# A convolution with a mixture of experts and an attention layer: normalising in two phases, and routing gates kept on chip

## The chip, the cores and the metric

The kernel runs on one core of one Trainium2 chip. The metric is the time of one launch on the device in microseconds (us), the median of several runs.

## What is computed

The input x is 32 images of 128 channels and 56 x 56 pixels, all in float32. Layer 0 is a block with a mixture of experts; layer 1 a 3 x 3 convolution (dilation 3), an attention over channels in the frequency domain and a gated branch. Cut to what matters here:

```python
# layer 0
x = depthwise_conv_7x7(input) + dw_bias                      # NCHW -> NHWC
x = (x - mean) / sqrt(var + 1e-6) * ln_gamma + ln_beta       # over the 128 channels
xf = x.reshape(T, C)                                         # T = 32*56*56 = 100352 tokens
topv, topi = top_k(xf @ Wg + bg, 2)                          # 8 experts, two for each token
wts = softmax(topv)
# each expert takes its cap = 1.25*T/8 tokens of highest wts[:, 0]; other pairs are dropped
y = gelu(xf[slot] @ W1[e] + b1[e]) @ W2[e] + b2[e]           # for every kept pair
moe = sum over the kept pairs of a token of  y * wts
x = input + x + layer_scale * moe
# layer 1
feat = gelu(batchnorm(conv3x3(x)));  F2 = fft2(feat)
attn = softmax of the channels' correlations in 8 heads
y = concat(|ifft2(attn @ F2)|, |ifft2(sigmoid(gate net of F2.real) * F2)|) + x
```

## The kernel before

**Convolution stage.** The images are taken in 8 groups of four. A group has 98 token columns of 128 tokens each (TG = 98; J = 784 columns in all), and its convolution is 16 steps `conv(g, c0, y)` of 8 channels. Each step loads an image tile `xt` (784 KB) and a weight tile `wt` (448 KB) from SyncE's queue (three buffers each), does 64 matmuls into two PSUM banks `psa`, and VectorE moves the banks into `y` with the bias added (L144). One group's `y` is [128 tokens, 98, 128 channels], with two buffers.

The rest of layer 0's work on a group, its normalising, its logits and its choice of experts, runs behind the convolution of the next group. `block` cuts the 98 columns into six blocks of 16 and one of 2, and gives five phases for each:

- `stats`: mean and variance on VectorE, a square root on ScalarE;
- `norm`: one ScalarE activation for every column (L181), then the affine part, a multiplication by gamma and an addition of beta on VectorE (L185), then the DMA of the token rows to the DRAM tensor `xf`, issued from ScalarE's queue (L188);
- `across`: TensorE transposes the columns (L196, tile `pyt`), ScalarE copies them to `yT`;
- `logits`: the matmul with Wg (tile `plq`), and ScalarE's copy;
- `back`: transposes back (tile `pl`), VectorE adds the bias into `lg`.

`plan` sets the order by hand: phase i of block b is issued after convolution step 3b/2 + i (rounded down) of the next group, and `choose` one step after the last phase, at step 14:

```python
for i, phase in enumerate(block(g, y, lg, t0, n)):
    at.setdefault(b * 3 // 2 + i, []).append(phase)
...
at[last + 1] = [lambda: choose(g, lg)]
```

Phases of a step follow the step's convolution in every engine's queue. After the last group they run without a convolution: the drain. `choose(g, lg)` finds the two best experts of every token and their weights, and writes `key`, which the search for the experts' thresholds reads. It also fills a tile `meta` with the two weights and the first expert's number, and stores it by DMA (L299) behind the tokens' rows: a row of `xf` has PITCH = 144 floats, 128 of them the token, 16 for `meta`, of which three are used.

**Expert stage.** First VectorE and TensorE search the thresholds (L416, L445) and make the list `ids` of expert 0's tokens; the later experts' searches and lists run in small pieces (`tick`) beside the experts. A chunk is 512 tokens, 31 chunks to an expert. `fetch` gathers the rows of the next chunk with four indirect DMAs of GpSimd (L671, tile `xg`, four buffers), TensorE transposes them (L677), and VectorE works out the chunk's gate with three small operations (L682, L690: which of the row's two weights belongs to expert e) and copies the transposes to `xT` (L691). `expert` does the two matmuls (L705 and L715) with the gelu between them (L708); VectorE adds b2 (L728) and multiplies by the gate (L734) into `yo`, which SyncE's queue stores to `yf`, a row for each slot.

**Layer 1.** Images go in 16 pairs; `front` makes the layer's input and its 3 x 3 convolution for the next pair while `back` transforms the present one. A row block `r` is 7 columns of 128 tokens (112 row blocks). `feed` places row block r, sums r + 1 and gathers r + 3. `gather(r)` loads the tokens' rows `xs` from `xf` (L845) and gathers the rows of both slots from `yf` into two tiles `y` with 14 indirect DMAs of GpSimd (L850, four buffers, that is, two row blocks). `total(r)` adds both to `xs`; `place` transposes the sum (L872) and adds it to the image (L877).

```python
def total(r):
    ...
    for y in ys:
        nc.vector.tensor_tensor(out=xs, in0=xs, in1=y, op=ALU.add)
```

The functions that the change touches, and their callers:

Of the kernel before, what the change touches and what calls it, by code (L numbers as in the profile page):

```python
# [37 lines left out]
C = 128  # L38
# [6 lines left out]
E = 8  # L45
# [9 lines left out]
CB = 8  # L55
PITCH = 144
BIG = 1.0e30
# [14 lines left out]
def conv_seq_kernel(ctx: ExitStack, tc: tile.TileContext, t: dict, out: bass.AP, dbg: dict):  # L72
# [28 lines left out]

    xf = dram.tile([J * 128, PITCH], F32, name="xf")
    yf = dram.tile([NSLOT + 1, C], F32, name="yf")
    xfv = xf.rearrange("(j p) c -> p j c", p=128)

    rkey = tc.tile_pool(name="rkey", bufs=1)
    rk = rkey.__enter__()
# [4 lines left out]
    with tc.tile_pool(name="a1", bufs=1) as a1, tc.tile_pool(name="a2", bufs=2) as a2, tc.tile_pool(  # L114
# [36 lines left out]
        def block(g, y, lg, t0, n):  # L151
# [26 lines left out]
            def norm():  # L178
                for i in range(n):
                    yi = y[:, t0 + i, :]  # L180
                    nc.scalar.activation(  # L181
                        yi, yi, AF.Identity, scale=sd[:, i : i + 1], bias=nb[:, i : i + 1]
                    )
                for w, op in ((gB, ALU.mult), (bB, ALU.add)):
                    nc.vector.tensor_tensor(  # L185
                        out=yb, in0=yb, in1=w.unsqueeze(1).broadcast_to([128, n, C]), op=op
                    )
                nc.scalar.dma_start(out=xfv[:, g * TG + t0 : g * TG + t0 + n, :C], in_=yb)  # L188

# [59 lines left out]

            return [stats, norm, across, logits, back]  # L250

        def choose(g, lg):
# [33 lines left out]
            m1, e1 = tops  # L286
            meta = a1.tile([128, TG, PITCH - C], F32, name="meta", tag="meta")
            nc.gpsimd.memset(meta, 0.0)  # L288
            w1, w2 = meta[:, :, 0], meta[:, :, 1]
            nc.vector.tensor_tensor(out=e1, in0=e1, in1=m1, op=ALU.subtract)  # L290
# [6 lines left out]
            nc.vector.tensor_tensor(out=w2, in0=e1, in1=m1, op=ALU.mult)  # L297
            nc.vector.tensor_copy(meta[:, :, 2], firsts[0][:, cut])
            nc.scalar.dma_start(out=xfv[:, cut, C:], in_=meta)  # L299
            hot = hots[0]  # L300
# [9 lines left out]

        NS = C // CB
        sizes = [16] * (TG // 16) + ([TG % 16] if TG % 16 else [])

        def plan(g, y):
            lg = a2.tile([128, TG, E], F32, name="lg")
            at = {}
            t0 = 0
            for b, n in enumerate(sizes):
                for i, phase in enumerate(block(g, y, lg, t0, n)):
                    at.setdefault(b * 3 // 2 + i, []).append(phase)  # L320
                t0 += n
            last = max(at)
            at[last + 1] = [lambda: choose(g, lg)]
            return at
# [35 lines left out]
    with tc.tile_pool(name="b1", bufs=1) as b1, tc.tile_pool(name="b2", bufs=2) as b2, tc.tile_pool(  # L360
# [301 lines left out]
        def fetch(e, ids, c0):  # L662

            ns = min(512, cap - c0 * 128)
            xg = c4.tile([128, 4, PITCH], F32, name="xg")
            xT = c2.tile([C, 512], F32, name="xT")
            gates = []
            pt = bank("pxt")
            for q in range(-(-ns // 128)):
                n = min(128, ns - q * 128)  # L670
                nc.gpsimd.indirect_dma_start(  # L671
                    out=xg[:n, q, :],
                    out_offset=None,
                    in_=xf,
                    in_offset=bass.IndirectOffsetOnAxis(ap=ids[:n, c0 + q : c0 + q + 1], axis=0),
                )
                nc.tensor.transpose(pt[:, q * 128 : q * 128 + n], xg[:n, q, :C], ident[:n, :n])  # L677
            gate = c4.tile([128, 4], F32, name="gate")
            gat2 = c4.tile([128, 4], F32, name="gat2")
            for n, q in spans(ns):  # L680
                for to, i, op in ((gate, 0, ALU.is_equal), (gat2, 1, ALU.not_equal)):
                    nc.vector.scalar_tensor_tensor(  # L682
                        out=to[:n, q],
                        in0=xg[:n, q, C + 2],
                        scalar=float(E - e),
                        in1=xg[:n, q, C + i],
                        op0=op,
                        op1=ALU.mult,
                    )
                nc.vector.tensor_tensor(out=gate[:n, q], in0=gate[:n, q], in1=gat2[:n, q], op=ALU.add)  # L690
            nc.vector.tensor_copy(xT[:, :ns], pt[:, :ns])  # L691
            return ns, xT, gate

# [6 lines left out]

        def expert(e, c0, ns, xT, gate, tick):
            hT = c2.tile([C, FF // C, 512], F32, name="hT")
# [23 lines left out]
            for n, q in spans(ns):  # L726
# [5 lines left out]
                    op=ALU.add,  # L732
                )
                nc.vector.tensor_tensor(  # L734
                    out=yo[:n, q],
                    in0=yo[:n, q],
                    in1=gate[:n, q].unsqueeze(2).broadcast_to([n, nq, C]),
                    op=ALU.mult,
                )
# [101 lines left out]
    def gather(r):  # L841
        if r >= NRB:
            return
        xs = d3.tile([128, NB, C], F32, name="xs")
        nc.sync.dma_start(out=xs, in_=xfv[:, r * NB : (r + 1) * NB, :C])  # L845
        ys = []
# [12 lines left out]
    def total(r):  # L859
        if r >= NRB:  # L860
            return
        xs, ys = rows[r]
        for y in ys:
            nc.vector.tensor_tensor(out=xs, in0=xs, in1=y, op=ALU.add)  # L864
# [442 lines left out]
```

## Time and profile before

| what | us |
|---|---|
| median of three runs (5589.1 to 5595.3) | 5591.9 |
| the profiled execution | 6457.2 |
| its span, from the first to the last instruction | 6455.5 |
| convolution beside the blocks' phases | 0 to 952 |
| drain: phases of the last group | 952 to 1067 |
| first search and list | 1067 to 1204 |
| experts | 1204 to 3370 |
| layer 1 | 3370 to 6455 |

The profile is of one execution and is read in this way. The stages in the table are cut at their first and last instructions in the timeline. The engines are PE (TensorE; PEld is its weight load), DVE (VectorE), ACT (ScalarE), POOL (GpSimd) and SP (SyncE); a name with q, as ACTq, is an instruction on that engine's queue that issues a DMA or handles a semaphore. A group of instructions is given by line, engine, operation, the tiles written and read, the count, and then the busy time, the mean time of one in ns, and the idle time of the engine just before it with what released it. "L850 POOL ... <-DVE xs L864" says that the gathers stood until the sums in line 864 were done. A line of waits has the engine and line that waited, for what, the time in all, the number of waits and the longest. A DMA queue has its packets, megabytes, and the share of the 16 DMA engines' time that it took. "Another core or an unknown queue" and "remote" stand for a wait whose releaser the profile doesn't show.

### The profile page before, as it was taken

What the parts mean: (1) busy time and instruction counts of PE and PEld (TensorE: products, weight loads), DVE (VectorE), ACT (ScalarE), POOL (GpSimd) and SP (SyncE); (2) the same over time, 40 slices, a digit from 0 to 9 for tenths busy, and PEclk for the clock granted to TensorE, in tenths of its full rate; (3) what the DMA queues carried; (4) which work ended last, traced back from release to release, by engine and by line L of the source; (5) the groups of instructions that cost most, each with busy time, mean ns of one, the idle gap of its engine ahead of it and who ended that gap; (6) DMA issues with size and microseconds to landing.
All of it is one profiled execution on the core that took longest, in us unless ns stands there. A gap on an engine that the chain in (4) does not pass through costs nothing.

```text
span 6455.5 us, 85506 instructions
## 1 busy us (share of the span) xinstructions
PE 4925.6 (76%) x32850; PEld 3344.5 (52%) x32850; DVE 3087.3 (48%) x6927; ACT 2090.8 (32%) x3595; POOL 2616.6 (41%) x2564
## 2 busy tenths in 40 slices
PE   6666653598887989999984677777776876777678
PEld 5555552376665756766762344434444443444445
DVE  4676675565656655345221334434443443444346
ACT  2445543132232323333330223333332333333235
POOL 0000000344353435444436645565555545555450
PEclk8888885799999999999996778888887887888789
DMA  9999983122222222222233233333333333333331
GB/s 229 220 233 214 227 201 83 36 65 62 52 67 51 70 54 69 68 70 72 70 110 70 64 83 99 92 85 75 96 94 84 96 91 82 81 93 95 83 97 44
DMA packets 616216, 634.08 MB, mean 98 GB/s; under 512 B 166145, under 2 KB 540546, under 8 KB 611714
## 3 DMA queue, kind: packets, MB, share of 16 engines
q1 hardware_dynamic: 332418, 395.64, 22.2%
q0 software_dynamic: 81664, 175.18, 12.7%
q10 hardware_dynamic: 201728, 57.81, 4.6%
q8 instruction: 260, 4.26, 0.3%
q14 instruction: 146, 1.20, 0.1%
HBM read 454.98 MB, written 173.41 MB: 97 GB/s over the span
## 4 chain that ended last, share of the span: by engine, by line
PE 35%; issue 14%; another core or an unknown queue 12%; POOL 11%; DVE 6%; ACT 3%; DMA 3%; DVEq 0%; POOLq 0%; ACTq 0%; SPq 0%
PE pf L895 8%; PE py L715 7%; PE ph L705 6%; POOL xg L671 6%; PE pm L939 5%; POOL y L850 4%; PE pt L931 3%; DMA xg<-xf,ids 2%; PE pg L963 1%; PE pxt L677 1%; PE pxs L872 1%; PE pim L1030 1%; DVE junk L416 1%; ACT oa L1043 1%
## 5 line engine op out<-in xcount | busy, mean ns | idle before, releaser
L850 POOL DMA_INDIRECT y<-yf,slot x1568 | 1640.2, 1046 | 1324.5 <-DVE xs L864 816.1
L671 POOL DMA_INDIRECT xg<-xf,ids x984 | 964.9, 981 | 1393.6 <-PE pxt L677 531.0
L895 PE MATMUL pf<-xp,cw 128*64 128x448 f32 x4032 | 1029.3, 596 | 186.1 <-issue 185.4
L708 ACT ACTIVATE hT<-ph,b1t 128x512 f32<-128x512 f32 (+1 forms) x992 | 673.3, 682 | 1468.7 <-PE ph L705 1282.1
L715 PEld LDWEIGHTS py<-W,hT 128*128 128x128 f32 x7872 | 951.5, 195 | 251.5 <-ACT hT L708 124.8
L715 PE MATMUL py<-W,hT 128*128 128x128 f32 x7872 | 1000.6, 281 | 98.9 <-DVE gat L682 41.7
L705 PE MATMUL ph<-xT,W 128*128 128x512 f32 (+1 forms) x1984 | 910.0, 598 | 6.6 <-issue 6.5
L895 PEld LDWEIGHTS pf<-xp,cw 128*64 128x64 f32 x4032 | 319.1, 146 | 732.9 <-issue 704.7
L933 DVE COPY mid<-pt 112x512 f32<-112x512 f32 (+3 forms) x480 | 307.4, 661 | 707.0 <-PE pt L931 327.1
L705 PEld LDWEIGHTS ph<-xT,W 128*128 128x128 f32 x1984 | 361.1, 194 | 346.6 <-issue 341.2
L136 PE MATMUL psa<-xt,wt 112*64 112x98 f32 x8192 | 424.2, 267 | 87.0 <-DMA wt<-in_wt_dram 74.8
L136 PEld LDWEIGHTS psa<-xt,wt 112*64 112x64 f32 x8192 | 400.9, 150 | 125.3 <-issue 66.9
L682 DVE SCALAR_TENSOR_TENSOR gat<-xg 128x4 f32<-128x4 f32 (+2 forms) x256 | 42.2, 165 | 780.6 <-DMA xg<-xf,ids 779.3
L288 POOL MEMSET meta<- 128x1568 f32 x8 | 11.2, 1406 | 958.2 <-DMA xf<-meta 851.7
L196 PE MATMUL pyt<-ident,y 128*128 128x128 f32 x784 | 154.7, 378 | 304.4 <-DVE nb L174 150.7
L942 ACT COPY T<-pm 128x464 f32<-128x464 f32 (+2 forms) x240 | 123.1, 520 | 643.2 <-PE pm L939 382.6
L864 DVE TENSOR_TENSOR xs<-xs,y 128x896 f32<-128x896 f32 x224 | 243.1, 1085 | 175.0 <-DMA y<-yf,slot 80.9
L181 ACT ACTIVATE y<-y,nb,sd 128x128 f32<-128x128 f32 x784 | 311.0, 488 | 16.9 <-DVE nb L174 16.9
L196 PEld LDWEIGHTS pyt<-ident,y 128*128 128x128 f32 x784 | 138.6, 201 | 331.1 <-issue 229.3
L144 DVE TENSOR_TENSOR y<-psa,dwbB 128x392 f32<-128x392 f32 x256 | 143.6, 563 | 327.7 <-PE psa L136 327.5
L1017 ACT COPY Q<-pm 128x464 f32<-128x464 f32 (+1 forms) x128 | 63.8, 511 | 692.1 <-remote 502.2
L877 DVE TENSOR_TENSOR xp<-xp,pxs 128x256 f32<-128x256 f32 x448 | 146.4, 383 | 255.3 <-remote 147.8
(376 smaller groups left out, 6479.1 us busy)
## 6 DMA issues: line engine op xcount, KB each, us to landing
xt<-in_x_dram SPq DMA_DIRECT2D x128, 784.0 KB
yf<-yo SPq DMA_DIRECT2D x240, 256.0 KB
xp<-in_xp_dram SPq DMA_DIRECT2D x32, 1832.0 KB
wt<-in_wt_dram SPq DMA_DIRECT2D x128, 448.0 KB
xs<-xf SPq DMA_DIRECT2D x112, 448.0 KB
xf<-y ACTq DMA_DIRECT2D x48, 1024.0 KB
y<-yf,slot POOLq DMA_INDIRECT x1568
out_dram<-oa SPq DMA_DIRECT2D x224, 112.0 KB
```

The costliest lines, as they stand in the source:

```text
L136: nc.tensor.matmul(ps[h * 64 : (h + 1) * 64, c * TG : (c + 1) * TG], lhsT=wt[:, c4 + c, b, :], rhs=xv[:, c4 + c, h, :, b * NB : b * NB + N ...
L181: nc.scalar.activation(yi, yi, AF.Identity, scale=sd[:, i : i + 1], bias=nb[:, i : i + 1])
L196: nc.tensor.transpose(pt[:, i * 128 : (i + 1) * 128], y[:, t0 + i0 + i, :], ident)
L671: nc.gpsimd.indirect_dma_start(out=xg[:n, q, :], out_offset=None, in_=xf, in_offset=bass.IndirectOffsetOnAxis(ap=ids[:n, c0 + q : c0 + q + ...
L705: nc.tensor.matmul(ph[:, :ns], lhsT=W1[:, e, f * C : (f + 1) * C], rhs=xT[:, :ns], start=True, stop=True)
L708: nc.scalar.activation(hT[:, f, :ns], ph[:, :ns], AF.Gelu, bias=b1t[:, e, f : f + 1])
L715: nc.tensor.matmul(py[:n, q * C : (q + 1) * C], lhsT=hT[:, f, q * 128 : q * 128 + n], rhs=W2[:, e, f, :], start=(f == 0), stop=(f == FF // ...
L850: nc.gpsimd.indirect_dma_start(out=y[:, m, :], out_offset=None, in_=yf, in_offset=bass.IndirectOffsetOnAxis(ap=s[:, r * NB + m : r * NB + ...
L864: nc.vector.tensor_tensor(out=xs, in0=xs, in1=y, op=ALU.add)
L895: nc.tensor.matmul(pf[i * DD : (i + 1) * DD, : 8 * W], lhsT=cw[:, k, :], rhs=xps[i][:, o : o + 8 * RP].rearrange("p (h w) -> p h w", w=RP) ...
L933: dve(mid[:m, :ni, :].rearrange("p i c -> p (i c)"), pt[:m, : ni * 128])
L939: nc.tensor.matmul(pm[:, i * M : (i + 1) * M], lhsT=mid[:m, i, :], rhs=by, start=True, stop=True)
```

## The change

Two things change. First, the phase `norm` is cut in two: the ScalarE activations stay in `norm`, and the affine part with the rows' DMA becomes a phase of its own, `affine`. The phases of a block are put at steps 0, 1, 3, 4, 5 and 6 after its first, so that `affine` comes two steps after `norm`, `across` one step after that, and `choose` falls to step 16, after the last convolution step. Second, the gates are no longer stored with the rows. Their two weights go into two tiles that stay on chip, a row of `xf` is 128 floats, the experts' outputs are stored without their gates, and `total` multiplies each gathered tile by its gate before it adds it.

```diff
-PITCH = 144
-    xf = dram.tile([J * 128, PITCH], F32, name="xf")
+    xf = dram.tile([J * 128, C], F32, name="xf")
+    gates = [route.tile([128, J], F32, name=f"gate{r}") for r in (1, 2)]
 ...
             def norm():
                 for i in range(n):
                     ...
+
+            def affine():
                 for w, op in ((gB, ALU.mult), (bB, ALU.add)):
                     nc.vector.tensor_tensor(
                         out=yb, in0=yb, in1=w.unsqueeze(1).broadcast_to([128, n, C]), op=op
                     )
-                nc.scalar.dma_start(out=xfv[:, g * TG + t0 : g * TG + t0 + n, :C], in_=yb)
+                nc.scalar.dma_start(out=xfv[:, g * TG + t0 : g * TG + t0 + n, :], in_=yb)
 ...
-            return [stats, norm, across, logits, back]
+            return [stats, norm, affine, across, logits, back]
 ... choose:
-            meta = a1.tile([128, TG, PITCH - C], F32, name="meta", tag="meta")
-            nc.gpsimd.memset(meta, 0.0)
-            w1, w2 = meta[:, :, 0], meta[:, :, 1]
+            w1, w2 = gates[0][:, cut], gates[1][:, cut]
 ...
-            nc.vector.tensor_copy(meta[:, :, 2], firsts[0][:, cut])
-            nc.scalar.dma_start(out=xfv[:, cut, C:], in_=meta)
 ... plan:
+        BEHIND = 0, 1, 3, 4, 5, 6
-                for i, phase in enumerate(block(g, y, lg, t0, n)):
+                for i, phase in zip(BEHIND, block(g, y, lg, t0, n)):
                     at.setdefault(b * 3 // 2 + i, []).append(phase)
 ... fetch:
-            xg = c4.tile([128, 4, PITCH], F32, name="xg")
+            xg = c4.tile([128, 4, C], F32, name="xg")
-            gate = c4.tile([128, 4], F32, name="gate")
-            gat2 = c4.tile([128, 4], F32, name="gat2")
-            for n, q in spans(ns):
-                ...
-            return ns, xT, gate
+            return ns, xT
 ... expert:
-                nc.vector.tensor_tensor(
-                    out=yo[:n, q],
-                    in0=yo[:n, q],
-                    in1=gate[:n, q].unsqueeze(2).broadcast_to([n, nq, C]),
-                    op=ALU.mult,
-                )
 ... total:
-        for y in ys:
+        for y, gate in zip(ys, gates):
+            gate = gate[:, r * NB : (r + 1) * NB].unsqueeze(2).broadcast_to([128, NB, C])
+            nc.vector.tensor_tensor(out=y, in0=y, in1=gate, op=ALU.mult)
             nc.vector.tensor_tensor(out=xs, in0=xs, in1=y, op=ALU.add)
```

## Prediction

> **What bounds the kernel now.** I read the page first, for the slices and the chain. Then a table of windows cut the span into its stages, and in each stage I asked the waits, the DMA queues and the timeline. This is the table of windows (us; busy time and instructions of each engine, clock, DMA share, GB/s):
>
> ```profile
> core 0: us, PE busy (x) PEld busy (x) DVE busy (x) ACT busy (x) POOL busy (x), PEclk, DMA share, GB/s
> 222.00:837.00 615.00, 399.42 (x6002) 348.86 (x5999) 417.32 (x1106) 294.85 (x695) 7.03 (x5) 0.82 0.94 225
> 952.00:1067.00 115.00, 38.55 (x174) 26.20 (x174) 72.66 (x200) 60.21 (x140) 1.40 (x1) 0.61 0.26 63
> 1204.00:3370.00 2166.00, 1996.95 (x11262) 1451.22 (x11262) 1098.90 (x2775) 680.28 (x999) 964.89 (x984) 0.96 0.27 65
> 3370.00:6455.00 3085.00, 2245.18 (x11920) 1300.42 (x11920) 1220.91 (x2128) 937.28 (x1484) 1640.22 (x1568) 0.82 0.34 86
> ```
>
> Four stages, four limits. The convolution (to 952) has its DMA engines 94% busy. The drain of the last group (952 to 1067) has nothing over 63%: a serial chain. The experts (1204 to 3370) have TensorE 92% busy. Layer 1 has TensorE 73%, GpSimd 53%, VectorE 40%: a mesh of waits.
>
> The convolution works in periods: the gate DMA is issued at 222.06, then four periods later at 714.20 and at 836.84, so a group takes 122.96 us. The DMA view of these five periods, and TensorE's waits in them:
>
> ```profile
> q1 hardware_dynamic: 20541, 101.22, 61.5%
> q10 hardware_dynamic: 126080, 36.13, 31.7%
> PE pyt L196 <- DVE nb L174: 86.2, 15, 13.4
> PE pyt L196 <- ACT y L181: 39.3, 5, 7.9
> PE pyt L196 <- DVE df L168: 35.4, 4, 9.3
> PE psa L136 <- DMA wt<-in_wt_dram: 32.6, 20, 2.7
> ```
>
> q1 is SP's (taps and images), q10 is ScalarE's (token rows and gates). TensorE waits 176 us at the transposes pyt (with two smaller rows, 9.5 and 5.1; 35 per group) for a block that is still being normalised, and 33 us for weights: while it stands, the three load buffers fill and DMA goes quiet; afterwards DMA is saturated.
>
> The drain and what follows it, from the timeline around 1067 (start, length, instruction, idle before it and its releaser):
>
> ```profile
> 1067.06 1.47 DVE L302 TENSOR_TENSOR key<-hot,top 128x784 f32<-128x784 f32 x1
> 1067.28 0.37 ACTq L299 DMA_DIRECT2D xf<-meta  x1
> 1083.70 0.71 DVE L470 MEMSET onesj<- 128x784 f32 x1 [14.66 <-DMA xf<-meta]
> ```
>
> The last gate DMA holds up VectorE's first memset of the search for 14.66 us, with nothing beside it. For layer 1, the page's rows of the gathers and of the sums:
>
> ```profile
> L850 POOL DMA_INDIRECT y<-yf,slot x1568 | 1640.2, 1046 | 1324.5 <-DVE xs L864 816.1
> L864 DVE TENSOR_TENSOR xs<-xs,y 128x896 f32<-128x896 f32 x224 | 243.1, 1085 | 175.0 <-DMA y<-yf,slot 80.9
> ```
>
> GpSimd waits 816 us for the sums to free its row buffers.
>
> [...] alone, from about 1079, the gate DMA's 64-byte packets move 80 to 90 GB/s, where the taps reach 280. [...] a gather's median is 944 ns, but that at 4436.05 took 2.15 us beside a run of tensor-tensor additions. [...] L864's 1085 ns for 896 elements fits, so the new multiply costs the same. [...]
>
> **Which time the sum is made against.** The profiled execution took 6457.2 us (span 6455.5), 865 above the median of 5591.9. The chain of waits gives 12% of its span, 788 us, to "another core or an unknown queue", 33 us of it in one piece in most image pairs of layer 1 and almost none of it before 1204. I take the excess to lie there, so conv-stage savings carry over one to one, while layer 1 is tighter without the profiler: that matters for the price below.
>
> **Part 1, gates not written (conv stage).** Removed per group: one GpSimd memset (1.4 us, idle engine, worth nothing), a copy of 0.25 us, and a DMA of 12,544 packets. The last of these, nearly alone, made q10 59.3% busy for 17 us: 10.1 us of all 16 engines. Of the eight, six lie inside the convolution: 6 x 10.1 = 60 us of a resource that is 94% busy.
>
> **Part 2, normalising in two phases.** Nothing is computed anew. The two affine passes (2.28 us each on VectorE) and the row DMA on ScalarE's queue come two steps after the normalising, and the transposes three steps after it instead of one. Today ScalarE normalises block 0 from 476.95 to 483.2, its queue then holds until the affine is done (row DMA at 488.03, transposes behind it), copies the transposes, and starts block 1 at 493.52. With the change the next block's normalising stands behind it instead, and TensorE has convolution to do. Per group, DMA work is 0.939 x 122.96 = 115.5 us; less 10.1 leaves 105.4. At 100% busy a middle group takes 105.4, at today's 94% 112. I take 96%, 109.8: 13.1 saved, five times, is 66. The first period (96 to 222: 126 us, share 0.85, no gate DMA) becomes 112, the last (837 to 952: 115 us, share 0.87) 94: 14 and 21. Together **-100**, with Part 1 in it; ends -60 (gates alone) and -131 (full).
> A new wait: `choose` moves from step 14 to step 16, after the group's convolution, and its 15 us of VectorE stand ahead of the next group's evictions and statistics. VectorE then runs some 15 us, two steps of 7, late; three load buffers and eight PSUM banks cover about that. VectorE's 83 us per group stay below 110. If the cover is short, the gain falls towards the lower end.
>
> **Part 3, the drain.** Today from 952: 7 us left of `choose`, then ScalarE and VectorE in turns until 1053.5, then `choose` (to 1067). After: a whole `choose` ahead (+8). But 60 us of ScalarE work (39.0 normalising, 14.4 copies, 3.5) now overlaps 28.3 of affine and 20.4 of statistics. If ScalarE never waits, its 60 us follow the first block's statistics (timeline: 958.8 to 964.9, then the first normalising): about 65 us for what takes 94 (958.8 to 1053.5). Net **-21** (0 to -35). Gate DMA wait at 1083.7: **-14** (the rows' own last DMA was issued at 1051.25 and is long home).
>
> **Part 4, experts.** Removed per chunk from VectorE: three gate operations (0.16 each) and the multiply of yo (L734, 163.9 us over 240, 0.683 each): about 290 us in all. VectorE's 780 us of waits at gat for xg end with the transposes of the same chunk; they move to the xT copy, and TensorE sets the pace. What can gain is the change of expert for the first four: VectorE ends the list late (ids at 1770 where TensorE had finished at 1757.5). About 1.2 us less in each of the last 3.4 chunks is 4 us, four times: **-16** (0 to -45). Gathers of 512 instead of 576 bytes: nothing, DMA is 27% busy.
>
> **Part 5, layer 1.** Added: 2 x 112 multiplies of 1085 ns, 243 us of VectorE (40% to 47% busy). Two costs. Queue: behind each stand the mid copies; the view of L864 shows TensorE waiting 32.6 (pm) + 30.7 (pxs) us on it; doubling it is +63, and I charge half, 30, since TensorE has other work three quarters of the time. Port: gathers lose 1640.2 - 1568 x 0.944 = 160 us today to some 780 us of VectorE instructions with two SBUF inputs (groups by line: L864 243, L1046 135, L1123 129, L1035 68, L1088 and L1089 75, L1054 to L1094 131), 0.2 per us: 49 at that rate, 243 if every multiply stops GpSimd. I take 90, as sums stand where gather bursts begin, and charge half, 45. Together **+75**; ends 0 and +150.
>
> Sum: -100 - 21 - 14 - 16 + 75 = -76. Profiled 6381; median 5591.9 - 76 = **5516**.
>
> **Rivals.**
> (a) Layer 1 hides the multiplies: GpSimd's 816 us of waits speak for it, the 2.15 us gather against. -151: 5441.
> (b) Slower: the multiplies land on the path whole, because without the profiler's stalls gathering is the bound of layer 1: 1568 x (1.046 + 0.30 issue) is 2110 us, against a stage of some 2300 to 2400 (3085 less about 700 unknown). +243 - 151 = +92: 5684. It decides from 151/224 = 0.67 us of each 1.085. Against it: the profile shows GpSimd waiting, not leading.
> (c) The late `choose` makes VectorE the pace of the convolution, or the order written is not the order issued: the gain there is 60 and the drain's 0. -60 - 14 - 16 + 75 = -15: 5577.
>
> **How the numbers follow.** Main case 0.42, (a) 0.28, (b) 0.12, (c) 0.18. About 0.2% (11 us) is what a measurement can tell from no change. Main and (a) are faster, (b) slower; (c) spreads around -15: 0.11 faster, 0.05 same, 0.02 slower. Faster 0.81, same 0.05, slower 0.14. The range 5420 to 5600 holds the first two and most of (c).
>
> **What would show it.** Right: q10 at half its packets; groups near 110 us; pyt waits of TensorE under 10 us per group; DMA share 0.95 or more; no DMA wait before onesj; L850's mean up to 1.1 us; DVE 1460 us in layer 1. Wrong: groups of 118 or more with TensorE waiting for VectorE; layer 1 longer by over 150 us; or the conv stage unchanged in an execution without the profiler.

## The result and the profile after

The kernel after takes **6116.8 us** (median of 4 runs, 6114.7 to 6117.2), the kernel before beside it 5591.6 (5589.1 to 5595.3): ratio 1.094, 95% interval 1.092 to 1.096. The change makes the kernel 525 us slower; the prediction was 5516, and its range ended at 5600.

Kernel before takes 5589 to 5612 us on some chips and 6396 to 6530 us on others; I call them **the free and the held chips**, and every ratio here is against the kernel before on the same chip. The result above is from a free chip, but the profile of before (6457) from a held one, and no profile of the unchanged kernel before on a free chip was obtained.

The profile of after (span 6112.8 us, run 6114.7) is from a free chip: its chain of waits has no piece of "another core or an unknown queue". The table of windows, in the stages of the table shown for before:

```profile
core 0: us, PE busy (x) PEld busy (x) DVE busy (x) ACT busy (x) POOL busy (x), PEclk, DMA share, GB/s
222.00:837.00 615.00, 460.17 (x6830) 386.64 (x6828) 461.33 (x1209) 339.02 (x805) 0.00 (x0) 0.89 0.90 244
837.00:930.00 93.00, 40.62 (x186) 24.33 (x182) 66.54 (x189) 58.32 (x139) 0.00 (x0) 0.65 0.25 70
1077.00:3060.00 1983.00, 1952.90 (x11246) 1428.91 (x11245) 859.71 (x1727) 680.24 (x997) 957.30 (x975) 0.99 0.25 66
3060.00:6113.00 3053.00, 2201.99 (x11920) 1317.66 (x11920) 1434.06 (x2354) 923.00 (x1471) 1669.93 (x1568) 0.84 0.34 87
```

The same 615 us of convolution hold 6830 matmuls in place of 6002; the experts begin at 1077 in place of 1204 and take 1983 us with TensorE 98% busy. Layer 1 takes 3053 us, and there no engine is over 72% busy. Its length looks like that of before's profile (3085), but that one was of a held chip: a free kernel before has only about 2280 us left for layer 1 (5602.5 less 2 outside the span, less the 3321 at which a kernel with before's code up to there, e13 below, ends its experts). Layer 1 has lost some 775 us.

The DMA queues and TensorE's largest waits from 222 to 837:

```profile
q1 hardware_dynamic: 22528, 111.03, 66.9%
q10 hardware_dynamic: 74365, 37.73, 22.3%
PE pyt L198 <- DVE nb L174: 69.9, 11, 9.7
PE pl L222 <- ACT lq L217: 41.7, 18, 3.6
PE psa L136 <- DMA wt<-in_wt_dram: 33.8, 23, 2.2
```

q10 has lost its small packets, and the waits at the transposes pyt fell from 176 to 70 us. In their place TensorE waits 42 us at pl, the transposes back, a wait that the same view of before does not list. The start of the search has no DMA in front of it any more (timeline):

```profile
942.71 1.47 DVE L300 TENSOR_TENSOR key<-hot,top 128x784 f32<-128x784 f32 x1
944.54 0.71 DVE L469 MEMSET onesj<- 128x784 f32 x1
```

Layer 1, from the page's groups (busy and mean of one; idle time before them and what ended most of it):

```profile
L829 POOL DMA_INDIRECT y<-yf,slot x1568 | 1669.9, 1065 | 1260.9 <-DVE xs L845 755.3
L844 DVE TENSOR_TENSOR y<-y,gate 128x896 f32<-128x896 f32 x224 | 244.8, 1093 | 1298.1 <-DMA y<-yf,slot 1214.6
L845 DVE TENSOR_TENSOR xs<-xs,y 128x896 f32<-128x896 f32 x224 | 243.0, 1085 | 21.6 <-DMA xs<-xf 19.6
```

The multiply costs what was priced, 245 us of VectorE (1093 ns for one, where the add takes 1085). But VectorE stands idle ahead of it for 1215 us, until a gather has landed. The waiting has a consequence two rows up: GpSimd waits 755 us for adds to free a y. Before's profile has 81 and 816 us in these two places, but it is of a held chip; the figures to set beside 1215 and 755 are those of e14 below, 361 and 26, on a free one. The timeline shows how one wait makes the other:

```profile
4607.06 1.09 DVE L844 TENSOR_TENSOR y<-y,gate 128x896 f32<-128x896 f32 x1 [7.12 <-DMA y<-yf,slot]
...
4616.29 1.09 DVE L844 TENSOR_TENSOR y<-y,gate 128x896 f32<-128x896 f32 x1 [6.69 <-DMA y<-yf,slot]
...
4625.19 1.09 DVE L844 TENSOR_TENSOR y<-y,gate 128x896 f32<-128x896 f32 x1 [5.96 <-DMA y<-yf,slot]
...
4631.14 0.94 POOL L829 DMA_INDIRECT y<-yf,slot  x1 [0.30 <-issue]
4633.96 1.09 DVE L844 TENSOR_TENSOR y<-y,gate 128x896 f32<-128x896 f32 x1 [6.49 <-DMA y<-yf,slot]
4634.97 1.09 DVE L845 TENSOR_TENSOR xs<-xs,y 128x896 f32<-128x896 f32 x1
4636.33 1.49 POOL L829 DMA_INDIRECT y<-yf,slot  x1 [4.24 <-DVE xs L845]
...
4640.28 1.09 DVE L845 TENSOR_TENSOR xs<-xs,y 128x896 f32<-128x896 f32 x1
...
4662.17 1.07 DVE L845 TENSOR_TENSOR xs<-xs,y 128x896 f32<-128x896 f32 x1
...
4665.20 1.08 DVE L845 TENSOR_TENSOR xs<-xs,y 128x896 f32<-128x896 f32 x1
```

Four y's are multiplied at 4607, 4616, 4625 and 4634, as fast as seven gathers each arrive. All four buffers are then in use, and none is free: a y is freed by its add, and the first add stands behind the fourth multiply. GpSimd issues its last possible gather at 4631.14 and idles until the add of 4634.97.

This isn't chance. Counted in order, the multiplies at 4607 and 4616 belong to the adds at 4634.97 and 4640.28, and those at 4625 and 4634, of the *next* row block, to the adds at 4662 and 4665. So both multiplies of the next row block stand ahead of the adds of this one, and over the 224 pairs of the trace the multiply stands 26 VectorE instructions ahead of its add on average. The order is that of the compiled kernel: a second profile of after, on another chip (e9), has the same sequence of VectorE's 6119 instructions but for two. In the source each multiply is written just before its add, so the order issued is not the one written; and the multiply needs only y and the gate, while the add needs xs as well. In before, nothing could run on the gathered rows before xs was there: both adds of a row block stand with at most five instructions between them in its trace, and each wait for a gather is at the add itself.

### The profile page after: what moved, and what is told of

The parts are those of the page before. It is cut to its first block, busy times and chain, and to the rows that moved or that the text cites. A ratio compares the mean times of both kernels' runs of the same rounds, so it can differ in the third digit from the quotient of the medians.

```text
span 6112.8 us, 84264 instructions
## 1 busy us (share of the span) xinstructions
PE 4843.1 (79%) x32850; PEld 3320.7 (54%) x32850; DVE 3064.0 (50%) x6119; ACT 2071.0 (34%) x3580; POOL 2636.2 (43%) x2556
## 4 chain that ended last, share of the span: by engine, by line
PE 34%; POOL 25%; issue 21%; DVE 4%; DMA 2%; ACT 1%; POOLq 0%; SPq 0%; DVEq 0%; ACTq 0%
POOL y L829 25%; PE py L700 15%; PE ph L690 13%; PE pxt L675 2%; DMA y<-yf,slot 1%; PE pm L920 1%; DVE junk L415 1%; PE pf L876 1%; ACT y L181 1%; POOL xg L669 0%; PE pn L444 0%; DVE st L161 0%; DVE y L187 0%; PE pyt L198 0%; PE psa L136 0%
## 5 line engine op out<-in xcount | busy, mean ns | idle before, releaser
L829 POOL DMA_INDIRECT y<-yf,slot x1568 | 1669.9, 1065 | 1260.9 <-DVE xs L845 755.3
L700 PEld LDWEIGHTS py<-W,hT 128*128 128x128 f32 x7872 | 934.9, 191 | 143.6 <-issue 101.1
L700 PE MATMUL py<-W,hT 128*128 128x128 f32 x7872 | 981.1, 278 | 0.5
L876 PE MATMUL pf<-xp,cw 128*64 128x448 f32 x4032 | 949.3, 600 | 6.7 <-DVE xp L858 6.7
L844 DVE TENSOR_TENSOR y<-y,gate 128x896 f32<-128x896 f32 x224 | 244.8, 1093 | 1298.1 <-DMA y<-yf,slot 1214.6
L713 DVE TENSOR_TENSOR yo<-py,b2t 128x512 f32<-128x512 f32 (+2 forms) x256 | 170.6, 669 | 822.0 <-PE py L700 821.8
L920 PE MATMUL pm<-rw,mid 112*128 112x116 f32 x896 | 140.9, 309 | 226.6 <-DVE mid L914 226.6
L920 PEld LDWEIGHTS pm<-rw,mid 112*128 112x128 f32 x896 | 130.4, 224 | 230.8 <-issue 199.2
L845 DVE TENSOR_TENSOR xs<-xs,y 128x896 f32<-128x896 f32 x224 | 243.0, 1085 | 21.6 <-DMA xs<-xf 19.6
L920 PE MATMUL pm<-ih,mid 116*128 116x112 f32 x928 | 149.9, 315 | 106.0 <-DVE xp L858 56.9
L1024 ACT ACTIVATE oa<-feat 64x448 f32<-64x448 f32 x224 | 129.0, 576 | 281.4 <-DVE feat L1016 277.5
```

The lines of the kernel that those rows point to most:

```text
L700: nc.tensor.matmul(py[:n, q * C : (q + 1) * C], lhsT=hT[:, f, q * 128 : q * 128 + n], rhs=W2[:, e, f, :], start=(f == 0), stop=(f == FF // ...
L829: nc.gpsimd.indirect_dma_start(out=y[:, m, :], out_offset=None, in_=yf, in_offset=bass.IndirectOffsetOnAxis(ap=s[:, r * NB + m : r * NB + ...
L844: nc.vector.tensor_tensor(out=y, in0=y, in1=gate, op=ALU.mult)
L876: nc.tensor.matmul(pf[i * DD : (i + 1) * DD, : 8 * W], lhsT=cw[:, k, :], rhs=xps[i][:, o : o + 8 * RP].rearrange("p (h w) -> p h w", w=RP) ...
L920: nc.tensor.matmul(pm[:, i * M : (i + 1) * M], lhsT=mid[:m, i, :], rhs=by, start=True, stop=True)
```

## The experiments

**Theories.** *Early wait*: the multiply's place in VectorE's order is the cause, not its work. Rivals: *work and port* (245 us of VectorE passes, and gathers that they slow down, see Part 5 below), the *number of y buffers*, the convolution stage, and the 512-byte rows of xf. All times, each against the kernel before on its chip:

| Run | Kernel | us | before, us | ratio (95%) |
|---|---|---|---|---|
| e14 | after, multiply tied to xs | 5389.5 | 5603.2 | 0.961 (0.960 to 0.963) |
| e15 | before, y1+y2 first | 6242.2 | 5603.2 | 1.114 (1.112 to 1.116) |
| e16 | after, no multiply | 5340.1 | 5603.2 | 0.953 (0.951 to 0.955) |
| e13 | before, GpSimd clears y | 6254.6 | 5602.5 | 1.117 (1.114 to 1.120) |
| e12 | after, GpSimd clears y | 6330.8 | 5602.5 | 1.130 (1.127 to 1.134) |
| e1, e17 | before (profiles) | 6496.2, 6427.4 | 6497.6, 6425.7 | |
| e9 | after | 6412.6 | 6515.3 | 0.985 (0.982 to 0.987) |
| e4 | after, no multiply | 6320.6 | 6515.3 | 0.970 (0.967 to 0.973) |
| e2 | phases alone | 6424.1 | 6515.3 | 0.986 (0.982 to 0.990) |
| e3 | gates alone | 6514.7 | 6515.3 | 1.000 (0.998 to 1.002) |
| e5, e18 | after, multiply and add joined | 6396.8, 6324.7 | 6497.6, 6425.7 | 0.986 (0.983 to 0.988), 0.985 (0.981 to 0.988) |
| e6 | after, multiply on xs | 6302.1 | 6497.6 | 0.970 (0.967 to 0.973) |
| e8 | before, y1+y2 first | 6319.1 | 6497.6 | 0.972 (0.970 to 0.974) |
| e10 | after, multiply tied to xs | 6176.4 | 6497.8 | 0.950 (0.948 to 0.952) |
| e11, e19 | after, six y | 6366.8, 6328.3 | 6497.8, 6425.7 | 0.978 (0.975 to 0.981), 0.985 (0.981 to 0.988) |

The first five ran on a free chip, the others on held ones. The account of the result rests on the five; what the held chips show follows after them. The kernels without the multiply (e4, e16) and with it on xs (e6) compute another sum; they are there for their times alone.

### Same work, later place (e14, and e10 on a held chip)

```diff
         for y, gate in zip(ys, gates):
-            gate = gate[:, r * NB : (r + 1) * NB].unsqueeze(2).broadcast_to([128, NB, C])
+            tied = d4.tile([128, NB], F32, name="tied")
+            nc.vector.scalar_tensor_tensor(out=tied, in0=xs[:, :, 0], scalar=0.0,
+                in1=gate[:, r * NB : (r + 1) * NB], op0=ALU.mult, op1=ALU.add)
+            gate = tied.unsqueeze(2).broadcast_to([128, NB, C])
             nc.vector.tensor_tensor(out=y, in0=y, in1=gate, op=ALU.mult)
             nc.vector.tensor_tensor(out=xs, in0=xs, in1=y, op=ALU.add)
```

> The kernel with the tied multiply once more, for a chip where before takes 5591 to 5602 us (the last call met one): early-wait theory 5440 to 5600 us (before's time, less about 140 us up to the experts and 30 to 60 us in them, plus some 75 us of multiplies in layer 1); work-and-port theory 6050 us or more, as after (6117). Where before takes 6500 us it repeats 6176 us.

> The kernel after, with the same multiplies of y by the gate, but the gate's seven columns first pass through a small operation that reads xs (xs * 0 + gate, 128 x 7 elements, 224 of them), so that no multiply can be ordered ahead of its xs: it stands 3.7 VectorE instructions ahead of its add on average in place of 26. Where before takes about 6500 us, early-wait theory expects what the kernel with the multiply on xs took, 6290 to 6340 us (after: 6412), and work-and-port theory 6400 to 6450 us. Where before takes 5591 us, early-wait theory expects 5440 to 5600 us and work-and-port theory 6100 us or more.

5389.5 us: 727 us less than after (which ran on another free chip) with 224 small operations *more*, and 214 less than before. It is even below the range expected, since the experts gained more than was thought (see below). In its trace the multiply stands 3.7 instructions ahead of its add, in place of 26. The page of e14, and GpSimd's wait for adds:

```profile
L829 POOL DMA_INDIRECT y<-yf,slot x1568 | 1669.7, 1065 | 546.7 <-issue 489.1
L853 DVE TENSOR_TENSOR y<-y,tied 128x896 f32<-128x896 f32 x224 | 244.0, 1089 | 376.1 <-DMA y<-yf,slot 360.8
POOL y L829 <- DVE xs L854: 25.7, 13, 2.3
```

The multiplies take the same 244 us, and the gathers the same mean of 1065 ns. GpSimd's wait for adds, 755 us in after, is 26 here, and that difference, some 730 us, is the difference of the times (727). On the held chip e10 did better than its theory said (6176 for 6290 to 6340); why is not known.

### No work, early place (e15, and e8 on a held chip)

```diff
-        for y in ys:
-            nc.vector.tensor_tensor(out=xs, in0=xs, in1=y, op=ALU.add)
+        y1, y2 = ys
+        nc.vector.tensor_tensor(out=y1, in0=y1, in1=y2, op=ALU.add)
+        nc.vector.tensor_tensor(out=xs, in0=xs, in1=y1, op=ALU.add)
```

> The kernel BEFORE with y1 = y1 + y2 ahead of xs = xs + y1 once more, for a chip where before takes 5591 to 5602 us. No work is added, only an operation that needs nothing but the gathers, 43 VectorE instructions ahead of its partner. Early-wait theory: slower by 200 to 700 us. Work-and-port theory: the same as before within 20 us. Where before takes 6500 us it repeats 6319 us.

> The kernel BEFORE, with nothing added: its two adds for a row block take another order, y1 = y1 + y2 and then xs = xs + y1, in place of xs = xs + y1 and xs = xs + y2. 224 operations of the same size as before; but the first needs the gathered rows alone and stands 43 VectorE instructions on average ahead of the second. Early-wait theory: this alone makes the kernel slower by about what the change lost in layer 1, 5900 to 6300 us. Work-and-port theory: no work and no port time is added, 5580 to 5610 us as before.

This is the kernel *before* with as many operations as before, and it loses 639 us. Its first add, which needs no xs, stands 43 instructions ahead of the second. Work and port are ruled out as the main cause. Its waits:

```profile
DVE y L864 <- DMA y<-yf,slot: 1230.4, 112, 27.9
POOL y L850 <- DVE y L864: 362.2, 80, 9.6
POOL y L850 <- DVE xs L865: 325.9, 40, 15.7
```

VectorE again stands 1230 us ahead of gathers, and GpSimd waits 362 + 326 = 688 us for buffers. On the held chip the same kernel, with the same order of instructions, is *faster* than before by 2.8%, against its expectation; why is not known.

### No multiply (e16, and e4 on a held chip)

```diff
-        for y, gate in zip(ys, gates):
-            gate = gate[:, r * NB : (r + 1) * NB].unsqueeze(2).broadcast_to([128, NB, C])
-            nc.vector.tensor_tensor(out=y, in0=y, in1=gate, op=ALU.mult)
+        for y in ys:
             nc.vector.tensor_tensor(out=xs, in0=xs, in1=y, op=ALU.add)
```

> The kernel after without the multiplies (x + y1 + y2) once more, for a chip where before takes 5591 to 5602 us: both theories 5360 to 5450 us, the gain of all that the change does outside layer 1 (prediction: 151 us). If layer 1 is long without the multiplies too, as by the 512 byte rows of xf or by the gathers' own pace, 5700 us or more. Where before takes 6500 us it repeats 6321 us.

> The kernel after without the gates' multiplies: the sum takes y unscaled (x + y1 + y2). What is left of the change is the conv stage in two phases, the gates' rows that are no longer written to and gathered from DRAM, and the shorter VectorE work of the experts. Against before on the same chip this is the gain of everything but the multiplies; the prediction put it at 151 us (100 + 21 + 14 + 16). Both the early-wait theory and the work-and-port theory expect before minus 100 to 250 us. If the loss lay in the conv stage or in the 512 byte rows of xf instead, it would be there still: before plus 300 us or more.

5340.1 us: without the multiplies the change would gain 263 us, again more than expected. The rest of the change, with its 512-byte rows and its convolution stage, is not to blame, and the multiplies' whole price in their later place is 5389.5 - 5340.1 = 49 us. Its rows, and its layer 1 in the table of windows, show what bounds a free layer 1:

```profile
L829 POOL DMA_INDIRECT y<-yf,slot x1568 | 1640.5, 1046 | 523.3 <-issue 500.5
L843 DVE TENSOR_TENSOR xs<-xs,y 128x896 f32<-128x896 f32 x224 | 244.6, 1092 | 628.2 <-DMA y<-yf,slot 564.2
3071.00:5343.00 2272.00, 1979.04 (x11924) 1201.16 (x11922) 1212.52 (x2130) 946.21 (x1484) 1640.50 (x1568) 0.93 0.45 117
```

GpSimd gathers almost without a pause: 1640.5 busy and 500.5 of issue are 2141 of layer 1's 2272 us. **Gathering is the bound.** VectorE waits 564 us for gathers here too, and GpSimd hardly stands because of it, so a wait of VectorE is not a loss by its length alone.

One caution. In after, GpSimd's gathering, its issue and its wait for adds fill nearly all of layer 1 (1670 + 493 + 755 of 3053 us). Whatever made VectorE late would therefore show as this wait of GpSimd. The balance of 730 against 727 us shows where the time went; that the early order sent it there is shown by e14 and e15.

### More work for GpSimd (e13, e12)

```diff
             y = d4.tile([128, NB, C], F32, name="y")
+            for _ in range(4):
+                nc.gpsimd.memset(y, 0.0)
```

> The kernel BEFORE with work added to GpSimd alone: four clearings of y (128 x 896, some 0.8 us each by the 1.41 us that 128 x 1568 took) before its seven gathers, 896 in all and some 720 us of GpSimd's time in layer 1. In the stretched profile of before GpSimd issues up to 56 gathers in a row, one each 1.25 us, and in these rows the other engines come to a halt (from 4603 to 4620 us none of them starts an instruction while GpSimd issues 13 gathers). Starvation theory (long rows of gathers hold up the other engines, or the recording of them, and that is the 905 us between 5591 and 6497): pauses break the rows up and the kernel gets FASTER where before takes 6497 us, by 100 to 600 us, though work is added. If GpSimd's own pace bounds layer 1, it is slower by 300 to 700 us; if TensorE does, it is the same.

> The kernel AFTER with the same four clearings before each y's gathers. Where the early multiply makes gathering the path of layer 1 (25% of the chain of after is gathers), the 720 us of GpSimd's work lie on it: 6700 to 7100 us, and the distance to the kernel before with pauses shows what the early wait costs when the other engines aren't starved. If gathering isn't the path, it moves as the kernel before does with pauses.

The expectation of e13 speaks mostly of a held chip, but both ran on a free one, so its starvation theory was not tested. Before goes from 5602.5 to 6254.6, +652, for clearings that the page puts at 722.1 us: 90% of GpSimd's added work shows, which fits that gathering is the bound. After goes from 6116.8 (another free chip) to 6330.8, +214 for 727 us: neither outcome that was written down for it. Most of the work fills the pauses in which GpSimd stood for the adds (755 us without the clearings, 268 with them).

### The two parts alone (e2, e3)

e2 is before with the normalising in two phases and the steps of BEHIND (the lines that change, in part); e3 is after with these lines as in before:

```diff
+            def affine():
...
-            return [stats, norm, across, logits, back]
+            return [stats, norm, affine, across, logits, back]
...
+        BEHIND = 0, 1, 3, 4, 5, 6
...
-                for i, phase in enumerate(block(g, y, lg, t0, n)):
+                for i, phase in zip(BEHIND, block(g, y, lg, t0, n)):
```

> The kernel before with the first part of the change alone: normalising in two phases and the steps between a block's phases (0, 1, 3, 4, 5, 6); gates are written to DRAM and multiplied at the experts as before. Both theories put the loss in layer 1, which this leaves as it is: before minus 0 to 60 us. The prediction took the conv stage as bounded by the DMA queues, with 60 us of gate rows in it that this kernel keeps, and so gave the phases alone the other 40 of its 100 us.

> The kernel after with normalising in one phase and the old steps: the second part of the change alone. The multiplies stand 26 VectorE instructions ahead of their adds as in after. Early-wait theory: as after, within 20 us, plus what the phases save (0 to 60 us). If the phases were what slows the kernel, it is near before or faster.

Up to the experts a held chip runs as a free one (after: first expert matmul at 1076 free and 1077 held), so these runs tell of the convolution stage. By the first row DMA of each group in the timeline, over five groups, a group takes 123.0 us in before, 122.3 with the gates alone, 114.3 with the phases alone, 108.5 with both. Profiles of the same code differ here by over 1 us (121.7 in e15 to 123.1 in e1; 108.5 in after, 109.9 in e14), so the gates alone gained nothing that can be told apart. By their whole times both kernels missed what was expected: e2 gained 91 us in place of 0 to 60, and e3 is 102 slower than e9 in place of at most 80.

### Held chips (e1, e17, e9, e5, e18, e6, e11, e19)

e1 and e17 are the kernel before, e9 is after, unchanged. e5 and e18 join multiply and add column by column; e6 multiplies xs in place of y (the sum is then another one, with y unscaled); e11 and e19 have six y buffers and five of the ring's six.

```diff
# e5, e18
+            for m in range(NB):
+                nc.vector.scalar_tensor_tensor(out=xs[:, m, :], in0=y[:, m, :],
+                    scalar=gate[:, r * NB + m : r * NB + m + 1], in1=xs[:, m, :],
+                    op0=ALU.mult, op1=ALU.add)
# e11, e19 (y from d6; the ring has 5)
+    d6 = ctx.enter_context(tc.tile_pool(name="d6", bufs=6))
# e6
-            nc.vector.tensor_tensor(out=y, in0=y, in1=gate, op=ALU.mult)
+            nc.vector.tensor_tensor(out=xs, in0=xs, in1=gate, op=ALU.mult)
```

> The kernel before, unchanged, profiled once more. The prediction took the profiled execution of before (span 6455.5 us, 865 above its median) as stretched, by the 788 us that its chain lays to another core or an unknown queue, 700 of it in layer 1. If that was a disturbance of that one execution, this profile has a span near 5590 us, no such share in the chain, and layer 1 about 2385 us long with about 145 us for a pair of images. If the profile of this kernel is always so, the span is again near 6450 us with layer 1 near 3085 us, and the comparison of layer 1 with that of the kernel after (about 3050 us) has to be made by times alone.

> The kernel after, unchanged, beside the kernel before on the chip of this call. Kernel before has shown two times: 5589 to 5595 us in the four runs beside which after took 6117 us, and 6457 to 6506 us in its two profiled executions and in the runs of the last call, where the waits of ScalarE and VectorE name a remote releaser for 1750 to 1900 us in all; the profile of after names none. If the stretch is a property of the chip (or of where the program lies on it) that meets every kernel, after takes some 6900 to 7000 us where before takes 6490, and the ratio of 1.09 stands. If it meets only kernels whose engines are never stopped by something else, after takes about 6117 us in both places: it is slower than before where before runs free (5591) and faster where before is stretched (6490).

> The kernel after, with the gate's multiply and the add joined for each of a row block's seven columns: xs = y * gate + xs, 14 operations of 128 elements in place of 4 of 896. The product now needs xs, so no operation needs the gathered rows alone. Early-wait theory (the multiplies need only the gathers, are ordered 26 VectorE instructions on average ahead of their adds, and VectorE stands there 1215 us while the rows of y come free late): layer 1 falls back to its length before plus some tens of us, and the gains of the conv and expert stages show; 5300 to 5560 us. Work-and-port theory (245 us of added VectorE passes slow the gathers or lie on the path): the number of operations grows from 448 to 1568, with as much or more VectorE time, so 6000 to 6250 us. Buffer theory (y is held longer only because two operations in place of one have to read it): in between, 5700 to 5950 us.

> The kernel after, with the same multiplies on other data: xs = xs * gate in place of y = y * gate, each followed by the add of y. The sum is another one (x times both gates, y not scaled); the number, size and kind of VectorE operations and their two inputs are those of after. The first to wait for a gather is again the add, with no instruction between the two. Early-wait theory: the 1215 us of waiting at the multiply are gone, 5350 to 5600 us. Work-and-port theory: the work is all there, 6050 to 6150 us as the kernel after.

> The kernel after with six buffers of y in place of four (three row blocks in place of two) and, to make room, five of the ring's six buffers. The multiplies stand as far ahead of the adds as before or farther (44 VectorE instructions on average). If the loss comes from the four y buffers being held by multiplied rows that wait for their adds behind the next row block's multiply, the third row block lets the gathers run on: GpSimd's wait for the adds (755 us in the profile of after, 942 us in its run of the last call) falls by half or more and layer 1 gets shorter by 50 to 400 us. If the loss is that VectorE stands ahead of gathers, with mid copies behind it, it stays, within 30 us.

> The kernel before, unchanged, for a profile on a chip where it takes 5591 to 5602 us. By its time, less the 1213 us up to the experts and some 2030 to 2150 us of experts, layer 1 should take 2240 to 2360 us there, against 3053 us in the profile of after; no wait should name a remote releaser, and GpSimd's wait for the adds should be well under the 850 us of the stretched profiles.

> The kernel after with multiply and add joined column by column (1568 operations of 128 elements that all need xs), for a chip where before takes 5591 to 5602 us. Early-wait theory: like the tied multiply, which took 5390 us there: 5370 to 5450 us. If the number of small operations counts, each with its own wait, 5450 to 5700 us.

> The kernel after with six buffers of y and five of the ring, the multiplies as early as in after or earlier, for a chip where before takes 5591 to 5602 us. If the early multiply costs by holding the four buffers of y (GpSimd idles until the adds behind it free them), a third row block gives back half of the 727 us or more: 5400 to 5750 us. If VectorE's standing ahead of the gathers is what costs, or the order moves ahead with the buffers, it stays above 6000 us.

The expectations of e5, e6 and e8 took it for granted that before takes some 5591 us, and those of e17 to e19 were made for such a chip; none of them met one. Here after is 1.5% *faster* than before. Layer 1 (from the last expert matmul to the end) takes 3138 us in e1, 3242 in e9, 3148 without the multiply, 3125 with it on xs, 3006 in e10 and 2973 in e8, whose order is the early one: whatever the order, it is far above the 2272 of e16, and something other than the order holds it there. So the multiplies as the change has them cost 92 us there (e9 less e4, on one chip), where on a free chip they cost some 775 (after less e16). The multiplies' place still shows, in e6 and e10 against e9 by their ratios, but the joined form (e5, e18) gains nothing over after; that its 1568 small operations are the reason was not shown. Six y buffers gave 0.978 and 0.985, after 0.985: no sure gain, with the multiplies now 44 instructions ahead instead of 26. More buffers were not measured on a free chip. So it is shown that the early order costs the time; that it does so by holding the four y's, rather than by VectorE's other work standing behind the multiply, is read from the waits and the timeline and rests on no experiment with the buffers. What sets the two sorts of chip apart stays open.

## Why the prediction was wrong

Stage by stage, on free chips. No profile of before is free, so its stages are read from e13 and e15, which share its code up to the end of the experts. The first three rows compare e12 with e13, which ran on one chip and share the code of after and of before, each up to layer 1.

| Step of the sum | predicted | measured |
|---|---|---|
| convolution (Parts 1 and 2) | -100 | -101 (last convolution matmul ends at 945 in e13, 844 in e12) |
| drain (Part 3) | -21 | -11 (117 to 107) |
| wait for the gate DMA | -14 | -15 |
| first search and list | none | about +4 (128 in e13; 133 in e12, 131 in after) |
| experts (Part 4) | -16 | about -133 (2115 in e13 and 2119 in e15 to 1984) |
| layer 1 (Part 5) | +75 | about +775 |

The measured column sums to about +519 of the 525; its stages are read off several chips.

**Parts 1 and 2: the sum was right, its split was not, so the agreement is in part luck.** A group was to take 109.8 us and takes 108.5. But the gates, priced with 60 us of DMA time, bought 0.7 us a group alone, which the spread covers, and the phases 8.7 a group alone, where the whole is 14.5. The convolution of before wasn't bound by DMA, for all its share of 0.94: with the gates' packets gone (e3) the share falls to 0.81, and TensorE still waits 175 us at pyt, as in before. Only on top of the phases do the gates seem to count, with about 6 us a group. The forecast DMA share of 0.95 didn't come either (0.90), and pyt waits are about 12 us a group, not under 10. One reading was off without a part in the sum: in the view from 1079 to 1083.4 the gate DMA moves about 144 GB/s at first, and 84 to 95 only later. **Part 3** was half as large; choose in step 16 cost nothing that shows.

**Part 4 failed in size**, by 117 us. I priced only the instructions (4 us at each of four changes of expert) and said that VectorE's 780 us of waits at gat "move to the xT copy". They did not: the row of the xT copy has 19 us of waits in after. VectorE now waits at yo instead, 822 us, for matmuls that TensorE has yet to end. In before it stood ahead of every chunk's gather, and TensorE waited for it in turn. These rows of matmuls, of e13 and then of after, and e13's row of windows, to set beside the experts' row of after above, show it:

```profile
L715 PE MATMUL py<-W,hT 128*128 128x128 f32 x7872 | 988.7, 280 | 80.5 <-DVE yo L728 75.2
L700 PE MATMUL py<-W,hT 128*128 128x128 f32 x7872 | 981.1, 278 | 0.5
1206.00:3321.00 2115.00, 1976.49 (x11251) 1437.31 (x11250) 1091.12 (x2752) 682.99 (x999) 957.44 (x978) 0.97 0.27 66
```

TensorE's idle time in the stage falls from 139 us (2115 less 1976) to 30 (1983 less 1953). The gain belongs to the gates, not to the phases: on held chips the experts take 2153 us in e2, as in before (2144 to 2156 in its profiles), and 2094 in e3, as in e9 (2093). Which of the removed operations it was, those at gat or the multiply of yo, was not separated.

**Part 5 is the step that failed.** The work was priced well: 75 predicted, 49 measured in e14 against e16, and of it the port term of 45 was (1065 - 1046) ns x 1568 = 30 us; the gathers' forecast mean of up to 1.1 us holds, and VectorE's 1434 us in layer 1 are near the 1460 forecast. That VectorE's passes with two inputs in SBUF lengthen a gather shows in the timeline of before: the 842 gathers of layer 1 with no VectorE instruction beside them take 944 ns each (at most 957), the 154 beside copies of L933 alone 943, the 65 beside adds of L877 alone, which have one input in PSUM, 943 too, and the 86 beside sums of L864 alone 1220 on average. But layer 1 is longer by about 775 us in place of 75, far more than the 150 that were named as the sign of a wrong prediction. What was missing is the wait: some 727 us (after less e14) in which GpSimd stands for its buffers, put at nothing. I took the multiply to stand just ahead of its add, as the source has it, and charged half of TensorE's 63 us behind it. I never asked which semaphores the new instruction waits for by itself. In before the adds waited for xs and for gathers; the multiply has no xs in it, and the order has it a row block early.

**Rival (b)** had the right premise, that gathering bounds a free layer 1: its 2110 us are the 2141 of e16. I held against it that "the profile shows GpSimd waiting, not leading"; but that profile was of a held chip, and on a free one GpSimd has hardly any wait left (e16). Its mechanism was wrong all the same: in their later place the multiplies cost 49 us, so they don't lie on the path whole. And its end, +92, was far too low, since what goes on the path is not the multiplies' 243 us but the longer wait of GpSimd for its buffers.

**Rivals (a) and (c)**: the later multiplies still cost 49 us, so layer 1 doesn't hide them whole, and choose in step 16 made no group longer. The other half of (c), that the order written is not the order issued, is what came, but in layer 1 and not in the convolution where it was looked for.

**The execution that was argued from** was the last fault. I laid the profile's excess of 865 us to the profiler and took it to fall on both kernels alike. But it goes with the chip: on a free one the profiled execution of after takes as long as the others (6114.7 against 6116.4 to 6117.2), and on held ones all runs of before take 6396 to 6530. Nor is it alike: held, before loses some 900 us (5603 to 6498) and after some 300 (6117 to 6413). On held chips the forecast is near the mark, 5516 / 5592 or 0.986 against 0.985 measured, but by luck: there layer 1 lost about 104 us (e9 against e1) and the experts gained about 50. A sum made on a profile with 12% of unknown time held, here, for that condition at best.

## What to carry to other kernels

For every instruction that a change adds, list what it waits for by itself: where the order issued is not the one written, an operation with one dependency fewer than its neighbours can come ahead of them, as twice here (by 26 instructions in after, by 43 in e15), and the engine then stands in front of it (1215 and 1230 us) while the work behind it waits. Ask next which buffers its early result holds, and whether the engine that fills them is the bound: VectorE's 564 us of waiting in e16 left GpSimd hardly a pause, GpSimd's 755 us in after go with a loss of 727. A cheap false dependency (here 224 operations of 166 ns) can put the order right, and with it the change is worth 3.9% in place of costing 9.4%.

## What was unexpected of the hardware

In traces of held chips there are stretches in which no other engine starts anything while GpSimd issues gathers in a row: 17.5 us in before, from 4971.7, with 13 gathers, and 14 us in e17, from whose timeline these lines are:

```profile
4582.04 0.90 PE L1029 MATMUL pre<-feat,attn 128*128 128x448 f32 x1 [1.20 <-issue]
...
4590.65 0.94 POOL L850 DMA_INDIRECT y<-yf,slot  x1 [0.30 <-issue]
4596.09 0.70 ACT L1017 COPY Q<-pm 128x464 f32<-128x464 f32 x2 [33.16 <-remote]
4596.69 1.86 PE L1030 MATMUL pim<-feat,meanw 128*128 128x448 f32 x2 [13.74 <-ACT Q L1017]
```

From 4582 to 4596 no engine but GpSimd starts anything; ScalarE has stood for 33 us though its matmul had ended, and goes on 4.5 us after the last gather of the row. On the free chip GpSimd gathers with hardly a pause through all of layer 1 (e16), with TensorE 87% busy (1979 of 2272 us) beside it. Traces of held chips also hold fewer semaphore events: 38,000 to 41,000, against 72,000 to 75,000 in those of free ones (e9 and after, the same kernel: 39,792 and 72,506). No run here shows what makes them fewer, or whether it has to do with the halts.
